# A two-layer metaformer kernel: the convolution's first input in runs of eight channels, x as the first transfer, ordered spreads, and new order keys

## The chip, the core and the metric

The kernel runs on one core of a Trainium2 chip. The metric is the time of one execution on the device in microseconds (us). The core has five engines that run independently and meet at semaphores: PE (matrix products), DVE (vector), ACT (activations), POOL (a second vector engine), and SP, which here issues all the DMAs. A measurement of this kernel can tell about 0.5% from no change.

## What is computed

The input `x` has 8 images of 384 channels and 32 x 32 points, in fp32. Cut to what matters, the reference is:

```python
x = x + mamba(ln_c(x))               # layer 0, all 8 images
t = to_tokens(x); t = t + ffn(ln_t(t), W1, b1, W2, b2)
x = from_tokens(t)
x = x + conv(ln_c(x), offset)        # layer 1, all 8 images
t = to_tokens(x); t = t + ffn(ln_t(t), W1, b1, W2, b2)

# mamba: xz = x @ in_proj.T, a 3-tap convolution along the 1024 points, silu,
#        dt = softplus(...), then for each of 768 channels x 16 states
#        h = exp(dt * A) * h + (dt * u) * B;   y = sum_n h * C
#        y = (y + u * D) * silu(z);   return y @ out_proj.T
# ffn:   weights are replaced by the sign of (W - group mean); after each product
#        images 0..4 (5 groups of one image) are scaled by 128/absmax and clipped,
#        images 5..7 are set to zero; gelu lies between the two products
# conv:  each of 48 groups of 8 channels is displaced by whole points, then
#        filtered with a 5 x 5 gaussian of its own (border of zeros)
```

So only five images need the two ffn, while the scan and the convolution run for all eight. The gaussian separates in the two axes, so the convolution is two products along one axis each: for a group of 8 channels, a 32 x 32 matrix along y, and one along x.

## The kernel before, in words

**Work.** A unit is half an image (512 points); there are 16, and each passes through 6 blocks of 128 channels (j) and 4 groups of states (g): 384 scan steps. One step (`scan`, line 847) has, for each of two halves p, a product on POOL (`t <- dus * bc`, line 868), two decays on ACT (line 878) and two scans on DVE (line 893). It ends in a second product, on POOL for p = 0 (line 914) and on DVE for p = 1 (line 927), and a sum over states on PE into `y` (line 935). The tiles `t` have a ring of five buffers.

`prep` (line 803) computes dt (softplus, line 824) and dt * u (POOL, line 837) for two blocks ahead. `spread` (line 787) then lays each of them out for the scan: one transfer to DRAM (`via`) and eight back, four quarters q for each of the two halves p, into `dts` or `dus`.

**Around the scans.** The input projections (line 645), the output projection (`end`, line 997) and, for the last six units, the z part computed at the beginning and kept in DRAM (`early`, line 696; line 723). For the images 0 to 4, layer 0's ffn (products at lines 1386 and 1465), the convolution, and layer 1's ffn. For the images 5 to 7, the convolution alone (`rest`, line 1697). The sign of the weights is made once, in 20 pieces (`binarize`, line 1078; sign at line 1126).

**The convolution** (`conv`, line 1546). For each of three blocks c of 128 channels, points and channels change places four times:

1. DVE turns blocks of 32 x 32 of the normalised input so that partitions hold the point's x position and each row y holds 32 channels: `xt`, laid out as (y c) (line 1569).
2. PE multiplies by the first matrix, four groups of 8 channels per block (`ups`, line 1601). Each of its products reads 8 channels x 32 rows, in the order (c y): neighbours in the product lie 32 elements apart in `xt`.
3. DVE turns the result (line 1615), PE multiplies by the second matrix (`overs`, line 1629), DVE turns back (line 1642), and POOL adds the residual (line 1652).

Every fp32 product is two passes on PE, so that the profile counts 192 instructions of 256 columns for line 1601 (8 images x 3 blocks x 4 groups x 2).

**What sets the order.** The program is written as a list of operations. Each has an engine, a duration given by hand, the buffers that it reads and writes, an optional activation table, and a `key`. Before anything is issued, `Flow.run` plays the list through with these durations and takes, whenever an engine is free, the ready operation with the lowest key; the instructions are then written out in this order, and every engine runs its queue in it. Four rules matter here:

- A loop over the waiting operations, sorted by key and by the order of their making (line 291), takes the best:

```python
for i, (k, n, o) in enumerate(q):
    if best is not None and (k > best[0] or TIE and k == best[0]):
        break
```

  `TIE` is 0, so of ready operations with equal keys the one made last is taken. Most rings give out their buffers in order, so the first buffer of a ring must be opened before a later one.
- An operation whose table isn't the active one has `PEN` added to its key and may first be held back for a time by `HOLD` (line 159). An operation without a table is free of both; a load that it needs is then put in ahead of it when the program is compiled.
- SP issues a transfer only while fewer than eight are under way.
- Keys are counted in scan steps (0 to 384). A scan's operations have keys near the step (KB, KE, KC_, KY for POOL's first product, the decays, the second products and PE's sum). The other pieces have offsets (KP, KR for `prep`, KEND, KZ, KL, KX, KXP for what a unit does for the next, KG for the gate), `ROWS` gives the eight keys between which the stages of a row (an image's ffn, convolution, ffn) run, `CONVS` those of the three convolutions of the images 5 to 7, KI and KJ those of `binarize`, EZ0 and EZ1 those of `early`. AP, AD, AA, AL shift a row's keys by engine. `UNITS` adds four offsets for each unit.

The first transfers are made with key -60 (line 570): x's first unit, then the small vectors and matrices.

Of the kernel before, what the change touches and what calls it, by code (L numbers as in the profile page):

```python
# [36 lines left out]

KB, KE, KC_, KY, KG = -0.73, 4.53, 0.68, -3.95, -25.21  # L40

KP, KR = -4.7, 10.49
KEND, KZ, KL, KX, KXP = 1.3, 23.33, -31.97, -2.16, -4.45

KI, KJ = 196.21, 703.54
EZ, EZ0, EZ1 = 6, -56.93, 53.6

AP, AD, AA, AL = 41.75, -45.76, -50.69, -258.62

PEN = 8.61  # L50

GBS = 260.0


ROWS = [
    [15.34, -7.72, -143.06, 131.51, -3.17, 59.74, -84.96, -78.05],
    [94.3, 121.48, 131.64, -65.6, 211.87, 125.27, 265.88, 164.43],
    [164.72, 212.1, 341.92, 181.75, 145.72, 247.03, 303.52, 178.27],
    [227.6, 313.23, 335.93, 52.96, 178.3, 308.14, 239.43, 298.28],
    [299.47, 295.45, 361.88, 314.75, 306.17, 351.8, 603.44, 450.53],  # L60
]
CONVS = [
    [202.4, 111.11],
    [759.94, 953.69],
    [430.57, 41.38],
]


UNITS = [
    [0.0, 0.0, 0.0, 0.0],  # L70
    [0.0, 0.0, 0.0, 0.0],
    [0.0, 0.0, 0.0, 0.0],
    [0.0, 0.0, 0.0, 0.0],
    [0.0, 0.0, 0.0, 0.0],
    [0.0, 0.0, 0.0, 0.0],
    [0.0, 0.0, 0.0, 0.0],
    [0.0, 0.0, 0.0, 0.0],
    [0.0, 0.0, 0.0, 0.0],
    [0.0, 0.0, 0.0, 0.0],
    [0.0, 0.0, 0.0, 0.0],  # L80
    [0.0, 0.0, 0.0, 0.0],
    [0.0, 0.0, 0.0, 0.0],
    [0.0, 0.0, 0.0, 0.0],
    [0.0, 0.0, 0.0, 0.0],
    [0.0, 0.0, 0.0, 0.0],
]


# [65 lines left out]
class Flow:  # L154
# [1 line left out]


    SWITCH = 1.5
    HOLD = {"exp": 0.0, "silu": 8.77, "gelu": 2.31, "softplus": 0.0}

    def __init__(self, nc):
        self.nc, self.ops, self.key, self.filler = nc, [], 0.0, None
# [200 lines left out]
def metaformer_flow(ctx, tc, x, mw, f0, offset, f1, out):  # L363
    nc = tc.nc
    w_in, conv_w, conv_b, w_x, w_dt, b_dt, a_log, d_skip, w_out = mw
    fl = Flow(nc)
    op, dma = fl.op, fl.dma
# [64 lines left out]
    dus_r = ring("dus", [P, 2, T], 4)  # L432
# [129 lines left out]
    def load_x(i):  # L562
# [4 lines left out]
            return  # L567
        dma(lambda: t.ap, lambda: halves(x[b], s), (), [t], 768)

    fl.key = -60  # L570
    load_x(0)
    dma(lambda: cw.ap, lambda: conv_w.rearrange("(j p) t -> p j t", p=P), (), [cw], 10)

    def small(dst, src):
# [211 lines left out]

    def spread(src, r):

        via = via_r.new()
        dma(lambda: via.ap, lambda: src.ap, [src], [via])  # L790
        dst = [r.new(Q), r.new(Q)]
        for p in range(2):
            for q in range(Q):
                dma(
                    lambda p=p, q=q: dst[p].ap[q * D : (q + 1) * D],
                    lambda p=p: via.ap.rearrange("(c d) t -> d c t", d=D)[:, 2 * p : 2 * p + 2, :],
                    [via],
                    [dst[p][q]],
                    128,
                )  # L800
        return dst

    def prep(i, a):
# [204 lines left out]
    def state_space():  # L1008
        def at(i, j, g=0.0):
            fl.key = i * UNIT + j * NG + g  # L1010

        fl.key = -50
        ln(0)
        n0 = len(fl.ops)
        for j in range(JC):
            xin(0, j)
        weights.extend([o for o in fl.ops[n0:] if o.eng == "SP"][-1:])
        x_proj(0)
        n0 = len(fl.ops)
        load_bc(0, 0)  # L1020
        fl.key = -48
        prep(0, 0)
        started.extend(o for o in fl.ops[n0:] if o.eng == "SP" and o.key == -48)
        fl.key = -46
        n0 = len(fl.ops)
        for g in range(1, NG):
            load_bc(0, g)
        fl.key = -5
        zin(0, 0)
        zin(0, 1)  # L1030
        loads.extend(o for o in fl.ops[n0:] if o.wait == 0 or o.key == -46)
        for i in range(len(units)):
            nxt = i + 1 if i + 1 < len(units) else None
            for j in range(JC):
                for g in range(NG):
                    scan(i, j, g)
                    at(i, j, g)
                    if g == NG - 1 and j % 2 and i * JC + j + 1 < len(units) * JC:
                        fl.key += KP + UNITS[i][0]
                        prep(*divmod(i * JC + j + 1, JC))  # L1040
                        at(i, j, g)
                    if j == 0 and i > 0 and g == 0:
                        fl.key += KEND + UNITS[i][3]
                        end(i - 1)
                        at(i, j, g)
                    if j == 0 and g in (0, 2):
                        fl.key += KZ
                        zin(i, 2 + g)
                        zin(i, 3 + g)
                        fl.key -= KZ  # L1050
                    if nxt:
                        if j == 1 and g == 0:
                            fl.key += KL + UNITS[i][1]
                            load_x(nxt)
                            if nxt < LATE:
                                ln(nxt)
                            at(i, j, g)
                        if j in (2, 3, 4) and g in (0, 1):
                            fl.key += KX + UNITS[i][2]
                            xin(nxt, 2 * (j - 2) + g)  # L1060
                            at(i, j, g)
                        if j == 4 and g == 2:
                            fl.key += KXP + UNITS[i][2]
                            x_proj(nxt)
                            at(i, j, g)
                        if j == JC - 1:
                            load_bc(nxt, g)
                        if j == JC - 1 and g == 1:
                            fl.key += KZ
                            zin(nxt, 0)  # L1070
                            zin(nxt, 1)
                            fl.key -= KZ
                fl.key = i * UNIT + j * NG + NG + KG
                gate(i, j)
        end(len(units) - 1)


    def binarize(w, dst, kc, o):
# [6 lines left out]
        for g in range(NQ):  # L1085
# [40 lines left out]
                lambda e, z=z, s=s: e.activation(s.ap[:, :flat], z.ap[:, :flat], AF.Sign),  # L1126
                [z],
                [s],
            )
            op(  # L1130
                "POOL",
# [414 lines left out]
    def conv(src, dst, dst_ap):  # L1546

        xt = [hb_r.new(2) for _ in range(KC)]
        for s in range(NS):
            last = src is x1[B - 1] and s == NS - 1  # L1550
            if last:
                tn = st[len(units) - 1]["x1"]
            else:
                tn = tn_r.new()
                dma(
                    lambda tn=tn: tn.ap,
                    lambda s=s: halves(src.ap, s),
                    [src[s * KC + k] for k in range(KC)],
                    [tn],
                    768,  # L1560
                )
            layernorm(tn, 1e-6)
            ys = slice(s * T // 32, (s + 1) * T // 32)
            for c in range(KC):

                op(
                    "DVE",
                    0.7,
                    lambda e, c=c, tn=tn, ys=ys: e.transpose(
                        xt[c].ap.rearrange("p (y c) -> p y c", c=32)[:, ys, :],  # L1570
                        tn.ap[:, c, :].rearrange("p (y x) -> p y x", x=32),
                    ),
                    [tn],
                    [xt[c][s]],
                )
        for c in range(KC):
# [18 lines left out]
            for h in range(2):  # L1595
                acc = mm.new()

                def ups(e, lt=lts[0], acc=acc, h=h, c=c):
                    for k in (0, 1):
                        cs = slice(h * 16 + k * 8, h * 16 + k * 8 + 8)  # L1600
                        e.matmul(  # L1601
                            acc.ap.rearrange("p (c y) -> p c y", y=32)[:, k * 8 : k * 8 + 8, :],
                            lt.ap[:, 2 * h + k, :],
                            xt[c].ap.rearrange("p (y c) -> p c y", c=32)[:, cs, :],
                            start=True,
                            stop=True,
                        )

                op("PE", 1.0, ups, [lts[0], xt[c]], [acc], hold=[tr])
                hs = slice(h * T, (h + 1) * T)  # L1610

                op(
                    "DVE",
                    0.7,
                    lambda e, tr=tr, acc=acc, hs=hs: e.transpose(
                        tr.ap[:, hs].rearrange("p (c x) -> p c x", x=32),
                        acc.ap.rearrange("p (c y) -> p c y", y=32),
                    ),
                    [acc],
                    [tr[h]],  # L1620
                )
            for h in range(2):
# [3 lines left out]
                def overs(e, lt=lts[1], acc=acc, xs=xs, tr=tr):  # L1626
# [7 lines left out]
                            stop=True,  # L1634
                        )

                op("PE", 1.3, overs, [lts[1], tr], [acc])

                op(
                    "DVE",  # L1640
                    0.85,
                    lambda e, c=c, acc=acc, xs=xs: e.transpose(
                        xt[c].ap.rearrange("p (x y) -> p x y", y=32)[:, xs, :],
                        acc.ap.rearrange("p (c x) -> p x c", x=16),
# [3 lines left out]
                )  # L1648
            op(
                "POOL",  # L1650
                2.35,
                lambda e, xr=xr, c=c: e.tensor_add(
                    xr.ap.rearrange("p (y x) -> p y x", x=32),
                    xr.ap.rearrange("p (y x) -> p y x", x=32),
# [106 lines left out]
```

## Time and profile before

| | |
|---|---|
| three runs, us | 3698.68, 3707.25, 3713.39 (median 3707.25) |
| the profiled execution, us | 3705.44, its span 3703.7 |
| granted TensorE clock, mean | 0.923 of full speed |
| activation table loads | 391 planned at line 359, 5 elsewhere, 1.283 us each |
| DMA | 777 MB, 210 GB/s, 16 engines busy 74% |
| last scan product of POOL (line 868) | starts at 3621.8 us |

How to read the profile: the span is cut into engines' busy time. A group of instructions is given as line, engine and operation, output and input tiles, shapes, count, then the busy time, the mean of one in ns, and the idle time just before them with what ended it. Matmuls overlap in PE's pipeline, so the mean of one (for 128 x 512 about 0.6 us) is longer than the step from one to the next; that step is read from the trace in order of time, where a row such as "x12" gives the length of twelve in a row. The chain of waits is followed back from the last instruction, at each step to what released it.

### The profile page before, as it was taken

What the parts mean: (1) busy time and instruction counts of PE and PEld (TensorE: products, weight loads), DVE (VectorE), ACT (ScalarE), POOL (GpSimd) and SP (SyncE); (2) the same over time, 40 slices, a digit from 0 to 9 for tenths busy, and PEclk for the clock granted to TensorE, in tenths of its full rate; (3) what the DMA queues carried; (4) which work ended last, traced back from release to release, by engine and by line L of the source; (5) the groups of instructions that cost most, each with busy time, mean ns of one, the idle gap of its engine ahead of it and who ended that gap; (6) DMA issues with size and microseconds to landing.
All of it is one profiled execution on the core that took longest, in us unless ns stands there. A gap on an engine that the chain in (4) does not pass through costs nothing.

```text
span 3703.7 us, 35888 instructions
## 1 busy us (share of the span) xinstructions
PE 3189.1 (86%) x9572; PEld 1143.7 (31%) x9572; DVE 3086.6 (83%) x3080; ACT 2494.7 (67%) x3661; POOL 3157.0 (85%) x1680
## 2 busy tenths in 40 slices
PE   4777878987999897899979789998877999878988
PEld 1222223322333231333323233332223333323334
DVE  2798888878778889997987899889898888788986
ACT  4767886757667676677768757767665676765562
POOL 3879999897697998888899887989998788997893
PEclk7888979998999897999989899999988999988999
DMA  5858778696686886668587776969776787976964
GB/s 145 184 154 223 198 199 221 184 256 181 207 245 175 231 224 181 200 199 243 177 248 205 196 221 193 244 198 255 228 216 195 209 246 225 257 217 207 270 185 155
DMA packets 680820, 777.44 MB, mean 210 GB/s; under 512 B 113689, under 2 KB 434089, under 8 KB 680617
## 3 DMA queue, kind: packets, MB, share of 16 engines
q1 hardware_dynamic: 680616, 775.14, 74.4%
q8 instruction: 77, 1.26, 0.1%
q14 instruction: 127, 1.03, 0.1%
HBM read 578.45 MB, written 196.48 MB: 209 GB/s over the span
## 4 chain that ended last, share of the span: by engine, by line
PE 39%; DVE 16%; DMA 15%; POOL 12%; ACT 10%; issue 6%; SPq 2%; POOLq 0%; DVEq 0%; ACTq 0%
PE mm L1386 10%; PE mm L1465 9%; POOL t L868 8%; PE mm L645 6%; DVE dp L893 5%; PE y L935 4%; DMA dus<-via 3%; PE mm L997 3%; DVE t L893 3%; POOL t L914 3%; DVE t L927 3%; DMA dts<-via 2%; ACT L359 2%; ACT dp L878 2%; PE mm L1601 2%
## 5 line engine op out<-in xcount | busy, mean ns | idle before, releaser
L868 POOL TENSOR_TENSOR t<-dus,bc 128x1024 f32<-128x1024 f32 x768 | 1797.8, 2361 | 209.9 <-PE y L935 169.6
L914 POOL TENSOR_TENSOR t<-t,bc 128x1024 f32<-128x1024 f32 x384 | 906.8, 2362 | 99.6 <-DVE t L893 89.6
L935 PE MATMUL y<-t,sel 128*32 128x512 f32 x3072 | 554.9, 652 | 184.4 <-DVE t L927 117.8
L1465 PE MATMUL mm<-hb,w 128*128 128x512 f32 x1440 | 675.4, 609 | 28.4 <-DMA w<-w2d 12.1
L1386 PE MATMUL mm<-tn,w 128*128 128x512 f32 x1440 | 670.9, 611 | 24.7 <-DMA w<-w1d 7.5
L878 ACT ACTIVATE da<-dts,aneg 128x512 f32<-128x512 f32 x768 | 520.6, 684 | 240.7 <-DVE t L893 216.0
L878 ACT ACTIVATE dp<-dts,aneg 128x512 f32<-128x512 f32 x768 | 528.3, 688 | 207.2 <-DVE t L927 190.3
L893 DVE TENSOR_TENSOR_SCAN dp<-dp,h,t 128x512 f32<-128x512 f32 x384 | 491.3, 1279 | 71.7 <-ACT dp L878 53.5
L893 DVE TENSOR_TENSOR_SCAN dp<-dp,t 128x512 f32<-128x512 f32 x384 | 468.4, 1220 | 90.6 <-ACT dp L878 59.8
L893 DVE TENSOR_TENSOR_SCAN t<-da,h,t 128x512 f32<-128x512 f32 x384 | 481.2, 1267 | 64.2 <-POOL t L868 59.6
L893 DVE TENSOR_TENSOR_SCAN t<-da,t 128x512 f32<-128x512 f32 x384 | 458.2, 1206 | 79.5 <-POOL t L868 68.5
L359 ACT ACT_TABLE_LOAD x391 | 501.7, 1283 | 6.5
L645 PE MATMUL mm<-xn,win 128*128 128x512 f32 x900 | 439.3, 631 | 39.6 <-DMA win<-in_L_conv_in_proj_w 20.5
L927 DVE TENSOR_TENSOR t<-dp,bc 128x1024 f32<-128x1024 f32 x384 | 465.4, 1212 | 8.8 <-ACT h L920 4.0
L1465 PEld LDWEIGHTS mm<-hb,w 128*128 128x128 f32 x1440 | 264.9, 192 | 431.8 <-issue 352.7
L1386 PEld LDWEIGHTS mm<-tn,w 128*128 128x128 f32 x1440 | 269.4, 193 | 413.8 <-issue 311.5
L997 PE MATMUL mm<-z,wo 128*128 128x512 f32 x552 | 276.6, 634 | 12.2 <-DMA wo<-in_L_conv_out_proj_w 7.6
L645 PEld LDWEIGHTS mm<-xn,win 128*128 128x128 f32 x900 | 173.6, 200 | 294.7 <-issue 209.7
L1398 ACT ACTIVATE he<-mm,b 128x512 f32<-128x512 f32 x240 | 162.9, 680 | 148.9 <-PE mm L1386 141.6
L935 PEld LDWEIGHTS y<-t,sel 128*32 128x32 f32 x3072 | 83.4, 112 | 560.0 <-DVE t L927 201.1
L920 ACT COPY h<-dp 128x2 f32<-128x2 f32 x192 | 30.5, 159 | 218.4 <-DVE t L927 112.6
L1408 DVE TENSOR_REDUCE sm<-he 128x1 f32<-128x1024 f32 x120 | 144.3, 1203 | 30.8 <-ACT he L1398 30.2
(133 smaller groups left out, 3170.5 us busy)
## 6 DMA issues: line engine op xcount, KB each, us to landing
dts<-via SPq DMA_DIRECT2D x768, 128.0 KB, 4.4
dus<-via SPq DMA_DIRECT2D x768, 128.0 KB, 4.5
hd<-he SPq DMA_DIRECT2D x120, 512.0 KB, 4.7
hb<-hd SPq DMA_DIRECT2D x120, 512.0 KB, 5.9
via<-soft SPq DMA_DIRECT2D x192, 256.0 KB, 4.3
w<-w2d SPq DMA_DIRECT2D x120, 384.0 KB, 4.7
w<-w1d SPq DMA_DIRECT2D x240, 192.0 KB, 3.9
bc<-bcd SPq DMA_DIRECT2D x256, 128.0 KB, 4.7
```

Source lines behind the costliest of these rows:

```text
L359: nc.scalar.preload_act_table_set(SETS[table])
L645: e.matmul(acc.ap, w.ap[:, k, :], xn.ap[:, k, :], start=(k == 0), stop=(k == KC - 1))
L868: lambda e, t=t, du=du: e.tensor_mul(t.ap, du.ap, wide(0)),
L878: lambda e, c=c, r=r, dt=dt: e.activation(decay(c), dt.ap[:, r, :], AF.Exp, scale=aneg.ap[:, j * Q + c, g : g + 1],),
L893: e.tensor_tensor_scan(t.ap[:, r, :] if p == 0 else decay(c), decay(c), t.ap[:, r, :], 0.0 if s == 0 else hst[j][p].ap[:, g, r : r + 1], A ...
L914: op("POOL", 2.35, lambda e, t=t: e.tensor_mul(t.ap, t.ap, wide(1)), [bc], [t])
L927: lambda e, t=t: e.tensor_mul(t.ap, da[2].ap, wide(1)),
L935: e.matmul(y.ap[c * D : (c + 1) * D, :], sel.ap, ts[c // 2].ap[:, c % 2, :], start=(g == 0), stop=(g == NG - 1), tile_position=(0, c * D),)
L997: e.matmul(o.ap, flat()[:, j, :], zs[j].ap, start=(j == 0), stop=(j == JC - 1))
L1386: e.matmul(acc.ap, w.ap[:, k, :], tn.ap[:, k, :], start=(k == 0), stop=(k == KC - 1),)
L1398: lambda e, he=he, r=r, m=m, acc=acc: e.activation(he.ap[:, r, :], acc.ap, AF.Identity, bias=b1.ap[:, m : m + 1]),
L1465: e.matmul(acc.ap, w.ap[:, part * 2 + r, :], hs[m // 2].ap[:, r * T : (r + 1) * T], start=(m == 0), stop=(m == MC - 1),)
```

## The change

The same arithmetic is done; what changes is a layout, four entries in the order, and numbers.

- `conv`: `xt` is laid out as (k y c), with k the group of 8 channels. The first turn writes it in runs of eight channels, `ups` reads 256 neighbouring elements and leaves its result as (k y c), and the second turn reads that result in the new order. Four durations given by hand change with it.
- x's first unit gets the key -62.
- `spread`: the eight transfers back get keys by half, and within a half dts comes before dus. `started` takes in all of these keys.
- `binarize`: the sign has the table "exp".
- New values for nearly all the keys, for PEN and for two of HOLD; `UNITS`, all zeros before, is filled.

```diff
-KB, KE, KC_, KY, KG = -0.73, 4.53, 0.68, -3.95, -25.21
-KP, KR = -4.7, 10.49
-KEND, KZ, KL, KX, KXP = 1.3, 23.33, -31.97, -2.16, -4.45
-KI, KJ = 196.21, 703.54
-EZ, EZ0, EZ1 = 6, -56.93, 53.6
-AP, AD, AA, AL = 41.75, -45.76, -50.69, -258.62
-PEN = 8.61
+KB, KE, KC_, KY, KG = -0.75, 4.58, 0.61, -5.95, -30.47
+KP, KR = -4.65, 9.54
+KEND, KZ, KL, KX, KXP = 1.02, 21.54, -47.42, -1.4, -10.26
+KI, KJ = 309.46, 610.57
+EZ, EZ0, EZ1 = 6, -51.55, 13.22
+AP, AD, AA, AL = 40.07, -39.02, -62.25, -251.98
+PEN = 9.4
 ROWS = [
...
-    [299.47, 295.45, 361.88, 314.75, 306.17, 351.8, 603.44, 450.53],
+    [301.66, 303.08, 342.24, 221.3, 335.12, 332.46, 692.98, 479.37],
 ]
 CONVS = [
-    [202.4, 111.11],
-    [759.94, 953.69],
-    [430.57, 41.38],
+    [134.64, 46.36],
+    [817.98, 1032.39],
+    [390.16, -64.42],
 ]
 UNITS = [
-    [0.0, 0.0, 0.0, 0.0],
...
+    [1.76, 13.1, 0.04, -22.24],
...
-    HOLD = {"exp": 0.0, "silu": 8.77, "gelu": 2.31, "softplus": 0.0}
+    HOLD = {"exp": 0.0, "silu": 8.77, "gelu": 2.74, "softplus": 1.03}
...
+    fl.key = -62
+    load_x(0)
     fl.key = -60
-    load_x(0)
...
     def spread(src, r):
-        via = via_r.new()
+        via, k0 = via_r.new(), fl.key
         dma(lambda: via.ap, lambda: src.ap, [src], [via])
         dst = [r.new(Q), r.new(Q)]
         for p in range(2):
+            fl.key = k0 + 0.02 * p + (0.01 if r is dus_r else 0.0)
             for q in range(Q):
                 dma(
...
+        fl.key = k0
         return dst
...
-        started.extend(o for o in fl.ops[n0:] if o.eng == "SP" and o.key == -48)
+        started.extend(o for o in fl.ops[n0:] if o.eng == "SP" and -48.5 < o.key < -47.5)
...
                 lambda e, z=z, s=s: e.activation(s.ap[:, :flat], z.ap[:, :flat], AF.Sign),
                 [z],
                 [s],
+                table="exp",
...
-                        xt[c].ap.rearrange("p (y c) -> p y c", c=32)[:, ys, :],
-                        tn.ap[:, c, :].rearrange("p (y x) -> p y x", x=32),
+                        xt[c].ap.rearrange("p (k y c) -> p y k c", k=4, c=8)[:, ys],
+                        tn.ap[:, c, :].rearrange("p (y a b) -> p y a b", a=4, b=8),
...
                     for k in (0, 1):
-                        cs = slice(h * 16 + k * 8, h * 16 + k * 8 + 8)
                         e.matmul(
-                            acc.ap.rearrange("p (c y) -> p c y", y=32)[:, k * 8 : k * 8 + 8, :],
+                            acc.ap[:, k * 256 : k * 256 + 256],
                             lt.ap[:, 2 * h + k, :],
-                            xt[c].ap.rearrange("p (y c) -> p c y", c=32)[:, cs, :],
+                            xt[c].ap[:, (2 * h + k) * 256 : (2 * h + k + 1) * 256],
...
-                op("PE", 1.0, ups, [lts[0], xt[c]], [acc], hold=[tr])
+                op("PE", 0.75, ups, [lts[0], xt[c]], [acc], hold=[tr])
...
-                        tr.ap[:, hs].rearrange("p (c x) -> p c x", x=32),
-                        acc.ap.rearrange("p (c y) -> p c y", y=32),
+                        tr.ap[:, hs].rearrange("p (k c x) -> p k c x", k=2, x=32),
+                        acc.ap.rearrange("p (k y c) -> p k c y", k=2, c=8),
...
-                op("PE", 1.3, overs, [lts[1], tr], [acc])
+                op("PE", 1.2, overs, [lts[1], tr], [acc])
                 op(
                     "DVE",
-                    0.85,
+                    0.7,
...
                 "POOL",
-                2.35,
+                2.85,
```

The three changes of a duration at the end belong to `overs`, to the last turn (line 1642) and to POOL's sum (line 1652).

## The prediction

> **What bounds the kernel now.** I read the page first, its busy shares and its chain of waits.
>
> ```profile
> PE 3189.1 (86%) x9572; PEld 1143.7 (31%) x9572; DVE 3086.6 (83%) x3080; ACT 2494.7 (67%) x3661; POOL 3157.0 (85%) x1680
> PE 39%; DVE 16%; DMA 15%; POOL 12%; ACT 10%; issue 6%; SPq 2%; POOLq 0%; DVEq 0%; ACTq 0%
> ```
>
> Three engines stand at 83 to 86% and none is full. The chain passes from one to the next and lies on PE for 39% of the span. So a microsecond taken from PE is worth between nothing and itself. Next, busy time by stage (columns: start, end and length, then PE, PEld, DVE, ACT, POOL busy).
>
> ```profile
> 0.00:100.00 100.00, 49.05 (x103) 15.11 (x104) 26.46 (x33) 46.44 (x72) 32.79 (x41) 0.76 0.61 150
> 300.00:900.00 600.00, 507.75 (x1511) 179.62 (x1508) 505.78 (x495) 443.98 (x647) 551.55 (x282) 0.91 0.78 212
> 900.00:1900.00 1000.00, 898.74 (x2733) 325.73 (x2731) 848.90 (x831) 699.68 (x1027) 848.15 (x444) 0.95 0.73 209
> 1900.00:2900.00 1000.00, 859.28 (x2586) 301.46 (x2584) 869.26 (x874) 671.23 (x997) 896.31 (x482) 0.93 0.78 219
> 2900.00:3600.00 700.00, 630.96 (x1907) 229.63 (x1908) 597.44 (x602) 461.38 (x654) 614.73 (x322) 0.94 0.78 228
> 3600.00:3704.00 104.00, 87.98 (x305) 41.51 (x303) 68.74 (x87) 24.34 (x35) 46.79 (x21) 0.95 0.46 153
> ```
>
> The start (one scan pair by 100 us) and the last 104 us, which hold the last scans and a convolution, are poorly filled. Between them POOL is busy from 84.8% (900:1900) to 91.9% (300:900) with the same kinds of work. That spread is what an order of the instructions can be worth.
>
> **Part 1: the convolution's first product.** The groups by line, then PE's instructions in order of time (start, length).
>
> ```profile
> L1601 PE MATMUL mm<-hb,lt 128*128 128x256 f32 x192 | 89.2, 615 | 13.0 <-DVE hb L1569 8.4 <-DVE hb L1642 4.1 <-DVE xn L498 0.5
> ...
> 2160.22 5.31 PE L645 MATMUL mm<-xn,win 128*128 128x512 f32 x12
> 2165.37 7.09 PE L1601 MATMUL mm<-hb,lt 128*128 128x256 f32 x16
> ...
> 2174.87 3.83 PE L1629 MATMUL mm<-hb,lt 128*128 128x128 f32 x32
> ```
>
> Back to back, 512 columns in one run take 5.31/12 = 0.443 us. The 256 columns of L1601, read 32 elements apart, take 7.09/16 = 0.443 us too, so twice as long per column. L1629's 128 columns, in runs of 16, take 3.83/32 = 0.120 us and pay no such factor. After the change L1601 reads 256 neighbours: 0.221 us (half of the first) to 0.240 (twice the last), I take 0.23. Saved on PE: 192 x (0.443 - 0.23) = 41 us; bounds 0 and 43. Following the chain in windows of 100 us, L1601's pieces add up to 72 us, 16.3 of them after 3600. Shortened by 48%, that chain would lose 35 us, but a second one (POOL's products, the scans) is close behind everywhere except in the tail. I take 20 us, half of PE's 41, near PE's 39% of the chain: 6 to 8 of it in the tail, where L1601 alternates with short turns, the rest in the middle.
>
> The turns beside it. L1615 now reads the accumulator 8 elements apart and L1569 writes in runs of 8. [...]a doubled L1615 would cost 48 x 0.71 = 34 us of DVE.
>
> ```profile
> L1615 DVE STREAM_TRANSPOSE hb<-mm 128x512 f32<-128x512 f32 x48 | 33.8, 706 | 24.2 <-PE mm L1601 21.7 <-ACT mm L529 2.4
> L1642 DVE STREAM_TRANSPOSE hb<-mm 128x512 f32<-128x512 f32 x48 | 32.8, 692 | 6.3 <-PE mm L1629 6.1 <-ACT da L878 0.2
> ```
>
> L1642 reads the same kind of accumulator 16 apart at 692 ns, not above the 706 of the contiguous L1615. So the row says 0, and I take 0 (bounds -1 and +34). No row shows the split write of L1569. The nearest is its own 677 ns; bounds 0 and +32 us if it doubled, taken 0. Both would lie on DVE, which is 83% busy and no cover: about half of any such cost would reach the end.
>
> **Part 2: x first.** SP's queue at the start:
>
> ```profile
> 0.74 0.98 SPq L217 DMA_DIRECT2D wdt<-in_L_conv_dt_proj_w  x1
> ...
> 4.62 0.54 SPq L217 DMA_DIRECT2D cw<-in_L_conv_conv_w  x1
> 5.20 0.55 SPq L217 DMA_DIRECT2D xn<-in_x  x1
> ```
>
> Ops of equal key leave in the reverse order of their making (the loop of line 291 keeps the last of equals), so x, made first, was eighth. At key -62 it goes at about 0.74, that is 4.46 us earlier. The chain runs from x's landing (10.73) through the layernorm to the first projection at 26.88 without slack, and `ones` and `pick` are ready at 3.1. The seven transfers that it passes move 0.55 us later; their first readers come late (cw's at 32 us, wx's at 39, wdt's at 55). The whole start moves: -4.5 us, bounds 0 and -5.
>
> **Part 3: the spread.** The same reversal sent the second half's quarters before the rest of the first, and dus before dts:
>
> ```profile
> 65.72 1.26 SPq L217 DMA_DIRECT2D dts<-via  x3
> 67.08 5.99 SPq L217 DMA_DIRECT2D dus<-via  x8
> 73.36 2.66 SPq L217 DMA_DIRECT2D dts<-via  x5
> ```
>
> The scans use half 0 first. Put in order, its eight transfers go out in about 3.4 us (0.42 each) and land some 4.4 us later, near 73.5. The first L868 stood at 78.64, so that one step gains 5 us. What is late next is bc of the second group. Its twelve issues run from 80.71 to 93.9, behind the next spread and two loads of tn, and POOL waits 8.9 us for it until 97.92. Their number ahead is unchanged, so most of the 5 us is lost there: -1.5. In the middle, the waits put down to dus (8.6 us) and dts (16.5) are all there is to win: -4, bounds +5 (half 1 now late) and -15. On SP, half 0 of dus passes half 1 of dts, whose readers come one POOL product (2.36 us) later and wait for the previous pair anyway.
>
> **Part 4: the sign's table.** Three unplanned loads before the sign (L1126, 3.8 us) and one after it (1.3 us) become planned ones: -5 to +5 us on ACT. Together with the new penalty and holds, the number of loads may move from 391 by some tens. [...]
>
> ```profile
> 115.26 1.28 ACT L359 ACT_TABLE_LOAD   x1
> 116.56 0.63 ACT L732 ACTIVATE y<-y 128x512 f32<-128x512 f32 x1
> ```
>
> Here the next activation starts 1.30 us after the load, so 30 switches are 39 us by the row. [...]ACT at 67% hides most of it. I take -1, bounds -10 and +10.
>
> **Part 5: the keys.** All instructions stay and their order changes; no row shows the new order. Bounds from the stages: if the three later ones reached the 91.9% of POOL in 300:900, their 2359 us of POOL work would take 2567 us instead of 2700, -133. If the others fell to the 84.8% of 900:1900, they would take 50 + 57 + 25 = 132 more. Which side? The waits that order can change are long (POOL L868 for PE's y 169.6 us, its five buffers t being full; PE's y for L927 117.8). The durations by which the order is made now lie nearer to the rows: the sum at L1652 2.85 (2.35 before; the row says 2.88), the turn L1642 0.7 (0.85; 0.69), the first product 0.75 (1.0, where the row gives 4 x 0.443 = 1.77; about 0.92 after). Its error of 0.77 us on 48 ops, 37 us of PE lateness in bursts, shrinks to some 8. And y is asked for two steps sooner (KY). I take a quarter of the bound, -33, and call it the weakest term.
>
> **Sum.** 3705.4 (the profiled execution; span 3703.7) - 20 - 4.5 - 1.5 - 4 - 1 - 33 = 3641.4. The median of the three runs is 1.8 above the profiled one: 3643.
>
> **The rivals.**
> - *Order worth nothing, PE's saving hidden.* Only the start (4.5), the tail (7) and about 6 of the rest reach the end: 3690. For it: three engines are nearly level. Against it: L1601 is on the chain in its 72 us.
> - *Order worth most.* The later stages come near 91%: -33 becomes -100, giving 3576. For it: 300:900 shows it with DMA as busy. Against it: in 900:1900 PE is at 90%, which leaves little room for more.
> - *Slower: work left over for the end.* The last L868 ran at 3621.8; 82 us followed, by end, one convolution and a row's last stretch. The change sets one remaining convolution (CONVS[1]) from 760-954 to 818-1032 and the last row's last key from 450 to 479. Each convolution left over costs about 22 us of DVE (two layernorms at 3.5, six turns of 0.68, twelve of 0.70, sums) in a tail where POOL and ACT have nothing to overlap. It decides once over 62 us more than now is left after the last scan; with three or four convolutions, 70 to 90 us, the time is near 3730. Against it: a third key (CONVS[2]) moves the other way, and the tail's PE work shortens.
> - *A change that fails to do what it says.* If turns double, half of 66 us is lost: 3676, within the likeliest range.
>
> **How the numbers follow.** Likeliest case (3605 to 3680) 0.60; order worth most 0.14; hidden 0.17; slower 0.09. The measurement tells 0.5% apart, 18.5 us: 3688.7 and 3725.8. Faster = 0.60 + 0.14 + half of 0.17 = 0.82; same = the other half and a little of the slower case, 0.10; slower 0.08. The range 3575 to 3712 leaves out about half of the best case and the slower case.
>
> **What would show it.** L1601 near 0.23 us back to back and PE some 41 us less busy; L1615 and L1569 within 0.66 to 0.73; xn issued at 0.7 and the first projection near 22.4; dts and dus in fours at the first spread; no table load at L1126; the last L868 near 3565 with a tail under 80 us. I am wrong if POOL's share between 900 and 3500 stays at 87%, or if the last L868 comes earlier while the end does not.

## The result, and the profile after

The changed kernel takes 3735.6 us (median of five, 3727.0 to 3739.3), before 3700.2 (median of five, the three of the table above among them). The ratio is 1.0083, 95% interval 1.0066 to 1.0100: slower by about 31 us (the two medians lie 35 apart), where I had forecast 62 faster, and outside my range. Below, times of runs are medians too.

The page of the changed kernel (engines' busy time):

```profile
PE 3163.9 (85%) x9572; PEld 1147.3 (31%) x9572; DVE 3089.6 (83%) x3080; ACT 2477.2 (66%) x3646; POOL 3158.8 (85%) x1680
```

PE is 25 us less busy, DVE and POOL as before, ACT 18 us less (380 planned table loads instead of 391). The work shrank and the span grew by 30 us, so all of the loss is idle time. The mean granted TensorE clock was 0.915 instead of 0.923. A loss of this kind doesn't need a lower clock: a run below that differs from before by one number alone (1.01) is 2% slower at 0.920, and the layout alone is faster than before at the same 0.920. Where the loss arose is seen from the start of POOL's first product in each unit, read from both traces:

| start of unit | before, us | after, us | difference |
|---|---|---|---|
| 0 | 78.6 | 75.1 | -3.6 |
| 1 | 317.7 | 315.3 | -2.5 |
| 2 | 533.1 | 541.8 | +8.8 |
| 3 | 765.1 | 765.7 | +0.6 |
| 4 | 1006.0 | 1031.0 | +25.0 |
| 8 | 1888.8 | 1906.7 | +17.9 |
| 12 | 2732.4 | 2765.3 | +32.9 |
| last product | 3621.8 | 3659.4 | +37.6 |
| end of span | 3703.7 | 3733.8 | +30.2 |

The start gains 3.6, the tail behind the last scan gains 7.5 (82 to 74), both near the forecast. The middle, where I had expected to win, loses 41. On the way the difference comes and goes: it grows by 24 in the first 60 us of unit 3, is 10 at 892 us, 25 at unit 4 and 1 at 2186. Even one order drifts by up to 8 us between two executions (before and the run with 1.01, up to 1445 us). So the stretch in unit 3 shows how such a delay arises; it isn't a share of the final 30. POOL's groups there, first of the changed kernel (764 to 826, ten first products begun), then of before (764 to 811, twelve); the last columns are idle time before them and what ended it:

```profile
L871 POOL TENSOR_TENSOR t<-dus,bc 128x1024 f32<-128x1024 f32 x10 | 23.3, 2350 | 10.8 <-DMA dus<-via 8.8 <-DMA bc<-bcd 1.7 <-DMA w<-w2d 0.3
L917 POOL TENSOR_TENSOR t<-t,bc 128x1024 f32<-128x1024 f32 x5 | 11.7, 2355 | 3.4 <-DVE t L896 3.4
L1348 POOL TENSOR_SCALAR hb<-hb,sm 128x1024 f32<-128x1024 f32 x5 | 5.9, 1189 | 9.0 <-DMA hb<-hd 7.5 <-PE mm L1000 1.5
```

```profile
L868 POOL TENSOR_TENSOR t<-dus,bc 128x1024 f32<-128x1024 f32 x12 | 27.9, 2351 | 1.5 <-PE y L935 1.5
L914 POOL TENSOR_TENSOR t<-t,bc 128x1024 f32<-128x1024 f32 x5 | 11.8, 2355 | 1.7 <-DVE t L893 1.7
L1344 POOL TENSOR_SCALAR he<-he,sm 128x1024 f32<-128x1024 f32 x3 | 3.5, 1190 | 0.2 <-DVE sm L1337 0.2
```

And the order in which POOL stood there, in the changed kernel (start, length, and in brackets the idle time before):

```profile
769.49 1.19 POOL L1348 TENSOR_SCALAR hb<-hb,sm 128x1024 f32<-128x1024 f32 x1 [1.46 <-DMA hb<-hd]
771.26 2.35 POOL L917 TENSOR_TENSOR t<-t,bc 128x1024 f32<-128x1024 f32 x1 [0.58 <-DVE t L896]
774.13 1.19 POOL L1348 TENSOR_SCALAR hb<-hb,sm 128x1024 f32<-128x1024 f32 x1 [0.51 <-DMA hb<-hd]
776.78 1.19 POOL L1348 TENSOR_SCALAR hb<-hb,sm 128x1024 f32<-128x1024 f32 x1 [1.46 <-PE mm L1000]
781.29 1.19 POOL L1348 TENSOR_SCALAR hb<-hb,sm 128x1024 f32<-128x1024 f32 x1 [3.33 <-DMA hb<-hd]
782.75 2.34 POOL L871 TENSOR_TENSOR t<-dus,bc 128x1024 f32<-128x1024 f32 x1 [0.27 <-DMA w<-w2d]
...
825.85 2.34 POOL L871 TENSOR_TENSOR t<-dus,bc 128x1024 f32<-128x1024 f32 x1 [8.33 <-DMA dus<-via]
```

Read this as a queue. The clips of an ffn (L1348, ahead of its gelu) stand before the scan's products, and four of the five wait for their transfer of hd (7.5 us). POOL starts nothing else in these waits (1.46, 0.51 and 3.33 us in the rows above), and the products behind the clips start later. Each of the scans on DVE needs such a product. By the second product, at 782.75, unit 3 is 15 us behind; one wait for dus, 8.3 us at 825.85, brings it to 24. In the kernel before, this stretch had three clips of another kind that waited 0.2 us in all. Over the whole run the groups show more waiting for transfers. The changed kernel, then before:

```profile
L871 POOL TENSOR_TENSOR t<-dus,bc 128x1024 f32<-128x1024 f32 x768 | 1797.7, 2360 | 225.8 <-PE y L938 148.4 <-DMA bc<-bcd 27.5 <-DMA dus<-via 22.8
L1469 PE MATMUL mm<-hb,w 128*128 128x512 f32 x1440 | 683.4, 614 | 49.6 <-DMA w<-w2d 26.4 <-ACT hb L1445 8.7 <-DVE u L677 8.0
```

```profile
L868 POOL TENSOR_TENSOR t<-dus,bc 128x1024 f32<-128x1024 f32 x768 | 1797.8, 2361 | 209.9 <-PE y L935 169.6 <-DMA bc<-bcd 16.6 <-DMA dus<-via 8.6
L1465 PE MATMUL mm<-hb,w 128*128 128x512 f32 x1440 | 675.4, 609 | 28.4 <-DMA w<-w2d 12.1 <-ACT hb L1441 7.3 <-DVE xr L1000 3.1
```

The wait that I had hoped to shorten, for PE's y, did fall (169.6 to 148.4). POOL's share between 900 and 3500, which I had named as a sign, went from 87.3% to 86.4%.

The edits themselves came out as written. The convolution's first product and the turns of the changed kernel, by group and in order of time:

```profile
L1604 PE MATMUL mm<-hb,lt 128*128 128x256 f32 x192 | 57.2, 442 | 18.4 <-DVE hb L1573 7.3 <-DVE hb L1618 3.9 <-DVE tn L498 1.8
...
L1618 DVE STREAM_TRANSPOSE hb<-mm 128x512 f32<-128x512 f32 x48 | 33.1, 703 | 11.4 <-PE mm L1604 10.1
...
L1573 DVE STREAM_TRANSPOSE hb<-tn 128x512 f32<-128x512 f32 x45 | 28.7, 681 | 1.4 <-PE mm L1632 1.4
```

```profile
2230.96 1.99 PE L1604 MATMUL mm<-hb,lt 128*128 128x256 f32 x8 [0.81 <-DVE hb L1618]
```

The length of such a row includes the whole of its last product, 0.44 us here and 0.61 before. So the step from one start to the next is (1.99 - 0.44)/7 = 0.22 us; before it was (7.09 - 0.61)/15 = 0.43, a little less than the 0.443 that I read. Both turns kept their length (703 and 681 ns, before 706 and 677). At the start, x leaves first and the spread goes out in fours:

```profile
0.73 0.45 SPq L217 DMA_DIRECT2D xn<-in_x  x1
...
65.83 1.84 SPq L217 DMA_DIRECT2D dts<-via  x4
67.71 2.84 SPq L217 DMA_DIRECT2D dus<-via  x4
70.86 1.96 SPq L217 DMA_DIRECT2D dts<-via  x4
```

### The profile page after: what moved, and what is told of

Same layout as the page of the kernel before. It is cut to its first block, busy times and chain, and to the rows that moved or that the text cites. A ratio compares the mean times of both kernels' runs of the same rounds, so it can differ in the third digit from the quotient of the medians.

```text
span 3733.8 us, 35795 instructions
## 1 busy us (share of the span) xinstructions
PE 3163.9 (85%) x9572; PEld 1147.3 (31%) x9572; DVE 3089.6 (83%) x3080; ACT 2477.2 (66%) x3646; POOL 3158.8 (85%) x1680
## 4 chain that ended last, share of the span: by engine, by line
PE 30%; DVE 16%; DMA 11%; POOL 9%; ACT 6%; issue 5%; SPq 1%; POOLq 0%; DVEq 0%; ACTq 0%
PE mm L1469 9%; PE mm L1390 9%; POOL t L871 5%; DVE dp L896 5%; PE y L938 4%; DVE t L896 3%; PE mm L646 3%; PE mm L1000 3%; DVE t L930 2%; POOL t L917 2%; DMA w<-w1d 2%; ACT dp L881 2%; DMA dts<-via 1%; DMA dus<-via 1%; ACT L359 1%
## 5 line engine op out<-in xcount | busy, mean ns | idle before, releaser
L871 POOL TENSOR_TENSOR t<-dus,bc 128x1024 f32<-128x1024 f32 x768 | 1797.7, 2360 | 225.8 <-PE y L938 148.4
L1469 PE MATMUL mm<-hb,w 128*128 128x512 f32 x1440 | 683.4, 614 | 49.6 <-DMA w<-w2d 26.4
L938 PE MATMUL y<-t,sel 128*32 128x512 f32 x3072 | 541.4, 664 | 183.1 <-POOL t L917 90.9
L484 PE MATMUL mm<-sq,pick 96*128 96x512 f32 x208 | 133.1, 726 | 47.7 <-ACT sq L477 46.9
```

The costliest lines, as they stand in the source:

```text
L871: lambda e, t=t, du=du: e.tensor_mul(t.ap, du.ap, wide(0)),
L938: e.matmul(y.ap[c * D : (c + 1) * D, :], sel.ap, ts[c // 2].ap[:, c % 2, :], start=(g == 0), stop=(g == NG - 1), tile_position=(0, c * D),)
L1469: e.matmul(acc.ap, w.ap[:, part * 2 + r, :], hs[m // 2].ap[:, r * T : (r + 1) * T], start=(m == 0), stop=(m == MC - 1),)
```

## The experiments

Theory K: the new keys lose, the structure gains. Theory S: one of the structural edits loses. A third joined before the first runs, C, and became F after them: the keys fit one particular list, and any edit that the player sees reshuffles everything behind it.

**Layout alone, at the old order.** The changed accesses in `conv`, with the old durations, so that every engine gets its instructions in the order of before.

```diff
-    xt[c].ap.rearrange("p (y c) -> p y c", c=32)[:, ys, :],
+    xt[c].ap.rearrange("p (k y c) -> p y k c", k=4, c=8)[:, ys],
...
-    xt[c].ap.rearrange("p (y c) -> p c y", c=32)[:, cs, :],
+    xt[c].ap[:, (2 * h + k) * 256 : (2 * h + k + 1) * 256],
```

> The convolution's new layout alone, every instruction in the order of before (the hand-given durations are kept). Theory K (the new keys lose, the layout gains): 3670 to 3692 us, L1601's successor busy about 57 us instead of 89. Theory S (the edits of the structure lose): 3700 or more, the turns or the products slower than their rows. Theory C (the time hangs on the order so finely that each new order moves it by up to 1% either way): a gain near the prediction's 20, since here the order is the old one.

Measured: 3694.0 us, ratio 0.9973 (0.9964 to 0.9981), a gain of 10 us by the ratio (9 by the medians), less than theory K and theory C expected. The product's group of this kernel:

```profile
L1600 PE MATMUL mm<-hb,lt 128*128 128x256 f32 x192 | 55.7, 432 | 15.0 <-DVE hb L1569 8.3 <-DVE hb L1641 4.8 <-DVE xn L537 0.8
```

PE as a whole is 24 us less busy, and the end comes 10 us sooner. Nearly all of it comes from before the last scan (its last product 8.6 us earlier); the tail, 82 us, became 80.

**All structural edits, old keys.** The changed kernel with the constants of before.

```diff
-KB, KE, KC_, KY, KG = -0.75, 4.58, 0.61, -5.95, -30.47
+KB, KE, KC_, KY, KG = -0.73, 4.53, 0.68, -3.95, -25.21
...
-PEN = 9.4
+PEN = 8.61
...
```

> Layout with its new durations, x first, ordered spreads and the sign's table, with all keys, PEN and HOLD of before. Theory K: 3665 to 3690 us (20 from the layout, 4 from x, some from the spreads). Theory S: 3730 or more, as the changed kernel. Theory C: anywhere from 3660 to 3740, not near the sum of its parts.

Measured: 3780.0, ratio 1.0209 (1.0191 to 1.0227). Theory K falls: with the old keys the changed list is slower than with the new ones, by 44 us.

**New keys, old structure.** Before, with the constants of the changed kernel.

```diff
-KB, KE, KC_, KY, KG = -0.73, 4.53, 0.68, -3.95, -25.21
+KB, KE, KC_, KY, KG = -0.75, 4.58, 0.61, -5.95, -30.47
...
-PEN = 8.61
+PEN = 9.4
...
```

> The structure and durations of before with the new keys, UNITS, PEN and HOLD. Theory K: 3750 to 3770 us (the changed kernel's 3736 plus the lost gain of the structure). Theory S: near 3700. Theory C: anywhere from 3690 to 3770.

Measured: 3857.5, ratio 1.0411 (1.0391 to 1.0431), outside all three ranges. So each half of the change costs more than the whole: 77 and 155 us apart, 31 together.

**UNITS zero in the changed kernel.**

```diff
 UNITS = [
-    [1.76, 13.1, 0.04, -22.24],
+    [0.0, 0.0, 0.0, 0.0],
...
```

> The changed kernel with UNITS all zero. If the 64 new offsets are what loses (one form of theory K): 3700 or less. If the other keys lose: 3730 to 3750. Theory C: any of these, with the scan's delay at another place than after step 72.

Measured: 3797.6, ratio 1.0261 (1.0242 to 1.0279): taking the offsets out costs 62 us more, which no theory had in its range. They serve this list.

**x first, alone.**

```diff
+    fl.key = -62
+    load_x(0)
     fl.key = -60
-    load_x(0)
```

> The kernel before with one edit: x's first transfer at key -62; all other keys old. Theory F (the old keys fit one particular list, and any edit that the player sees reshuffles the order after it and costs 1 to 2%): 3730 to 3790 us although x lands 4 us sooner. Theory S (one of the edits has the cost by itself, the ordered spreads the first suspect): 3696 to 3702.

Measured: 3701.4, ratio 0.9996 (0.9982 to 1.0010). Theory F was too wide here: PE's, DVE's and POOL's instructions stood in the old order throughout, and ACT's but for two that changed places at 16 us, so this edit doesn't reshuffle. The first scan product is 3.9 us earlier; at the end nothing can be told from before (the interval holds -6.7 to +3.7 us).

**The ordered spreads, alone.**

```diff
+            fl.key = k0 + 0.02 * p + (0.01 if r is dus_r else 0.0)
             for q in range(Q):
...
+        fl.key = k0
```

> The kernel before with one edit: the spreads' transfers ordered by half and kind. Theory F: 3730 to 3790 us. Theory S: about 3780, the whole of the 78 us that all structural edits cost with the old keys. My prediction's own step: 3695.

Measured: 3877.2, ratio 1.0470 (1.0447 to 1.0494), above F's range and more than twice the loss of all structural edits together. So the spread isn't a cost that the others add to. In this kernel 75 us go in unit 4. Its busy times from 1150 to 1250 (the stretch and its length, then PE, PEld, DVE, ACT and POOL in us with their instructions, the granted clock, the DMA share and GB/s), and POOL's order inside:

```profile
1150.00:1250.00 100.00, 92.37 (x262) 35.83 (x255) 55.82 (x60) 64.09 (x89) 59.22 (x38) 0.97 0.54 161
```

```profile
1223.57 1.19 POOL L1346 TENSOR_SCALAR hb<-hb,sm 128x1024 f32<-128x1024 f32 x1 [3.13 <-DMA hb<-hd]
1226.31 1.19 POOL L1346 TENSOR_SCALAR hb<-hb,sm 128x1024 f32<-128x1024 f32 x1 [1.55 <-PE mm L1467]
1229.97 1.19 POOL L1346 TENSOR_SCALAR hb<-hb,sm 128x1024 f32<-128x1024 f32 x1 [2.47 <-DMA hb<-hd]
1234.92 1.19 POOL L1346 TENSOR_SCALAR hb<-hb,sm 128x1024 f32<-128x1024 f32 x1 [3.76 <-DMA hb<-hd]
```

PE is 92% busy, more than half of it (52 us) with the second ffn product, and POOL 59%. POOL waits 18 us in front of clips, the pattern of the changed kernel, and 18 more for DVE's scans. As I read it, such a stretch spends PE's work without the scan's beside it, and the scan's is then left for later.

**The sign's table, alone.**

```diff
                 [s],
+                table="exp",
             )
```

> The kernel before with one edit: the sign has the table exp. Theory F: 3730 to 3790 us. Theory S with the sign as the culprit: about 3780, and then table loads well above 391 and ACT's waits longer in the first 650 us only; else 3700.

Measured: 3811.7, ratio 1.0300 (1.0279 to 1.0322). This too is above F's range. Of the 110 us that it is behind, 14 are there at unit 2 and 101 at the last scan: spread over the run, also where no sign is made any more (the last is at 609 us). ACT has 419 table loads instead of 396 and is 36 us busier; whether that costs a part of the 110 wasn't tried. The ordered spreads alone, which change no table, have 412.

**Nothing but a number.** Two kernels, before with another hand-given duration; no instruction differs, only the order.

```diff
-                op("PE", 1.0, ups, [lts[0], xt[c]], [acc], hold=[tr])
+                op("PE", 1.01, ups, [lts[0], xt[c]], [acc], hold=[tr])
```

> The kernel before with the hand-given duration of the convolution's first product 1.01 instead of 1.0: no instruction, buffer or transfer differs, only the order that the player makes, from the first convolution on. Theory F: 3715 to 3780 us, equal to before up to the first convolution near 840 us. Theory S: 3700, within 0.3% of before.

Measured: 3772.9, ratio 1.0195 (1.0173 to 1.0218). POOL's, DVE's and ACT's instructions stand in the old order up to 1495 us, well past the first convolution (860 us); at unit 10 it is level with before (+0.2 us), at the last scan 64 us behind. POOL's product in this kernel:

```profile
L868 POOL TENSOR_TENSOR t<-dus,bc 128x1024 f32<-128x1024 f32 x768 | 1799.6, 2364 | 260.3 <-PE y L935 185.6 <-DMA dts<-via 42.9 <-DMA bc<-bcd 21.1
```

The second has 0.97 in the same place.

> The kernel before with the hand-given duration of the convolution's first product 0.97 instead of 1.0; nothing else differs. Theory F: slower than before by 1 to 2%, by another amount than the 1.01 (2.0%), since the order comes out different again: 3730 to 3780 us. If the 1.01 was a single misfortune: 3690 to 3715.

Measured: 3752.5, ratio 1.0133 (1.0113 to 1.0153).

**The same for the changed kernel.**

```diff
-                op("PE", 0.75, ups, [lts[0], xt[c]], [acc], hold=[tr])
+                op("PE", 0.76, ups, [lts[0], xt[c]], [acc], hold=[tr])
```

> The changed kernel with the duration of its first product 0.76 instead of 0.75; nothing else differs. Theory F, in the form that the new keys are fitted to the changed list as the old ones were to the old: 2 to 3% slower than the changed kernel, 3800 to 3850 us. If the new keys are a poor, ordinary set, as good as any: 3715 to 3760.

Measured: 3836.6, ratio 1.0357 (1.0331 to 1.0382), 101 us behind the changed kernel. A hundredth of a microsecond in the estimate of 48 operations makes the kernel before 71 us slower and the changed one 101; three hundredths the other way cost before 49. Every run that departs from the order of either kernel with its keys kept is slower than that kernel. That is what theory F says; how the two sets of keys were found isn't on record.

**The old layout at the new order.** The changed kernel with the accesses of before in `conv`, the new durations kept.

```diff
-    xt[c].ap[:, (2 * h + k) * 256 : (2 * h + k + 1) * 256],
+    xt[c].ap.rearrange("p (y c) -> p c y", c=32)[:, cs, :],
...
```

> The changed kernel with the convolution's old layout put back, at the order of the changed kernel (its hand-given durations are kept, so every instruction stands where it stood). Theory F (each list's keys are fitted to it; edits that leave the order alone add up): about 10 us slower than the changed kernel, 3746, as the layout gained 10 at the old order. If the layout is worth the 20 that I predicted where the new keys stand: 3756.

Measured: 3770.0, ratio 1.0175 (1.0152 to 1.0198). PE's, DVE's, ACT's and POOL's instructions stand as in the changed kernel, but for a few PE products that are recorded in another sequence. So the layout is worth 34 us at the new order and 10 at the old one; my expectation of equal gains fell, and why they differ wasn't tried. The new order, with the work of before, is 67 us worse than the old.

**Refitting.** The changed list with the products' durations set near the trace's, and keys moved by chance from the old ones as long as the player's list ended sooner. A part of the edit:

```diff
-KI, KJ = 309.46, 610.57
+KI, KJ = 241.90, 703.54
...
-    [301.66, 303.08, 342.24, 221.3, 335.12, 332.46, 692.98, 479.37],
+    [299.47, 295.45, 340.83, 314.75, 306.17, 346.56, 636.21, 398.60],
...
-                op("PE", 0.75, ups, [lts[0], xt[c]], [acc], hold=[tr])
+                op("PE", 0.95, ups, [lts[0], xt[c]], [acc], hold=[tr])
```

> The changed list (layout, x first, ordered spreads, sign's table), the convolution's two products given 0.95 and 1.0 as the trace has them, and keys that start from the old ones and were moved by chance a little at a time for as long as the player's own list ended sooner. Theory F (what lost is the fit of the keys to the list, not the list): 3690 to 3715 us, ahead of the changed kernel (3736) and far ahead of the same list with the unmoved old keys (3780). Theory L (the changed list itself, above all the ordered spreads, is worse to order): 3735 or more however the keys are moved.

Measured: 3718.0, ratio 1.0027 (1.0015 to 1.0038), just above F's range and below L's. The second, from another chance sequence:

> As k1, from another chance sequence: shows how far such a fit repeats. Theory F: within 15 us of k1, 3690 to 3725. Theory L: 3735 or more.

Measured: 3707.2, ratio 1.0001 (0.9987 to 1.0015). And the control on the old list and layout, with its durations set by the trace:

```diff
-                op("PE", 1.0, ups, [lts[0], xt[c]], [acc], hold=[tr])
+                op("PE", 1.8, ups, [lts[0], xt[c]], [acc], hold=[tr])
...
```

> The control: the old list and the old layout, durations by the trace (1.8 and 1.0 for the products, 0.7 for the last turn, 2.85 for the sum), keys moved in the same way for as long. Theory F: 3695 to 3725 us, so that list and layout differ by no more than the 10 to 34 us that the layout is worth at a fixed order. Theory L: 3690 or less, well ahead of k1 and k2.

Measured: 3720.9, ratio 1.0036 (1.0024 to 1.0048). Theory L falls: with other keys and two durations the changed list went from 3780 to 3718 and 3707, level with the old list refitted. That is with a layout worth 10 to 34 us, so at equal work its order may still be somewhat worse than the old one's, and no refitted kernel is ahead of before. The waits don't rank these orders. POOL's clips wait 5 us for hd in all three refitted kernels, as before (4.9), against 8.9 in the changed kernel and 23.0 with the ordered spreads alone; but with x first alone, at the time of before, they wait 9.8, and in the fastest kernel (next) 9.3. The product in the second refitted kernel waits longer for dus than the changed kernel's 22.8:

```profile
L871 POOL TENSOR_TENSOR t<-dus,bc 128x1024 f32<-128x1024 f32 x768 | 1796.7, 2360 | 236.8 <-PE y L938 167.6 <-DMA dus<-via 36.6 <-DMA bc<-bcd 10.3
L1348 POOL TENSOR_SCALAR hb<-hb,sm 128x1024 f32<-128x1024 f32 x120 | 141.8, 1192 | 9.8 <-DMA hb<-hd 5.3 <-PE mm L1469 3.8 <-PE mm L646 0.5
```

**What is ahead of both.** The two edits that leave the old order alone, together (the layout with the old durations, and x first; their diffs are above).

> The kernel before with the two edits that leave the old order alone: the new layout (old durations kept) and x as the first transfer. Theory F (at a fixed order such edits add up): 3686 to 3696 us, a ratio of 0.996 to 0.998, faster than before and after. If the microseconds gained at the start are lost again on the way: as e1 alone, 0.9973.

Measured: 3693.0, ratio 0.9972 (0.9957 to 0.9986). It is faster than before and after, and no faster than the layout alone; x's four microseconds are below what these runs can tell.

## Why the prediction was wrong

**The order (Parts 3 to 5): the step that failed.** I priced what changes the order as a sum of local gains: -1.5 and -4 for the spreads, -1 for the sign and -33 for the keys, together -39.5, or -44 with x first. In Part 5 I took the durations that lay nearer to the trace and the sooner y as reasons for a gain. The changed kernel with the layout of before shows the same sum at the same work: +67. What was missing is that each of these edits gives the player another list, and that the order that follows departs from the fitted one; I had put this cost at nothing.

How the 67 divides between the edits depends on what is changed first. With the old keys the structural edits, the layout among them, cost 77 us where I had -31; the new keys then win back 44. Given to the old list, the same keys cost 155. So the keys have no price of their own, and that 44 lies near my 33 is luck: the nearer durations, one of my two reasons, are in the kernel of 3780 us already. Alone, with the old keys, the ordered spreads cost 176 us and the sign 110. Their local effect is as I said: dts and dus in fours, no table load at the sign. My bounds for the order, -133 to +132 from the stages, were too narrow as well: two of these orders cost 155 and 176. What in an order makes the loss isn't shown; the two stretches above suggest that PE's and POOL's work no longer lie side by side.

**The layout (Part 1): right in kind, 20 taken, 10 at the old order and 34 at the new.** Its step of 0.22 us (0.23 taken) saves 192 x 0.21 = 40 us, close to the forecast's 41; PE as a whole is only 24 us less busy. The term was mis-sized in what reaches the end, and in opposite directions at the two orders. The turns' zero held for both open points (703 and 681 ns); the doubling in my bounds was an estimate that no run shows. Of the tail's 6 to 8, the old order shows 2; the 7.5 of the changed kernel belongs to another order's tail, and that it fits is luck.

**x first (Part 2): right at the start, lost behind it.** The first normalising product starts at 5.51 instead of 10.87, the first projection at 23.45 instead of 26.88. 2 us of the 5.4 go back there, since a transfer that I had not named is late next: aneg, for which ACT waits with the normaliser's logarithm (line 521) queued behind it.

```profile
20.16 0.28 ACT L618 ACTIVATE aneg<-aneg 128x96 f32<-128x96 f32 x1 [2.68 <-DMA aneg<-in_L_conv_A_log]
20.35 0.64 ACT L521 ACTIVATE mm<-mm,eps 128x512 f32<-128x512 f32 x1
```

**The rivals.** My slower case put the loss into the tail. The tail got shorter, and the loss lies in the middle. The rival that I lacked is the one that fits the runs: keys that suit one list, given another.

**Open.** Which property of an order costs the 30 us of the changed kernel stays open: one stretch (24 us from 766 to 826) shows how a delay arises, and more than half of it is gone again at 892; the sums of waits for hd and dus don't tell the good orders from the poor. The nearest to it that I found is PE's idle time before the second ffn product: 28 to 30 us in the four kernels at the old order, 37 to 46 in the refitted ones and 39 to 64 in all others; which comes first, the loss or the wait, isn't shown. Whether the lower granted clock (0.915) adds a part wasn't tried. Why the layout's gain differs between two orders wasn't tried.

## What to carry to other kernels

Where an order is made by a list player and its numbers were fitted, an edit has two prices: what it does to the work, and what it does to the fit. Measure the first at a fixed order (keep the durations that the player sees), and at the order that you mean to keep, since one layout gained 10 us at one and 34 at the other. Measure the second by a null edit that changes a number and no instruction. If the null moves the time by more than the gain that you hope for, refit before you judge. And when a sum of local costs is all that a forecast has, its range should be as wide as the null edit's effect, on the side of a loss above all.

## What the runs showed of the hardware that I had not expected

- Each of the two instructions that the profile counts for a product over 256 fp32 columns stepped in 0.43 us from start to start where the columns lie 32 elements apart, and in 0.22 where they lie side by side. With 128 columns in runs of 16 the step was 0.11 (3.83 us for 32 of them, the last one 0.29: 3.54/31). So a jump at every element doubled the step here, while runs of 16 took about as long per column as one run (0.89 and 0.86 ns); runs between 1 and 16 weren't tried.
- The 32 x 32 turn on DVE showed no such cost: one of 128 x 512 that reads PSUM in one run, 8 or 16 elements apart took 706, 703 and 692 ns, one that writes SBUF in runs of 8 took 681 against 677.
